# A two-layer relational graph convolution: groups of 512 nodes in a circular buffer of 1536, and steps ordered by tile numbers

## The chip, the cores and the metric

The kernel runs on one core of a Trainium2 chip. The metric is the device time of one execution in microseconds (us). "Before" is the kernel as it stood, "after" is the changed one.

## What is computed

Two layers of a relational graph convolution over N = 50,000 nodes with 128 features, 16 relations and 8 bases, and a layer normalization of the input plus the result. There are 850,000 edges, sorted by destination: 800,000 random ones and a self loop for each node.

```python
def layer(h, src, dst, rel, basis, w_comp, loop_w, bias):
    W = einsum('rb,bio->rio', w_comp, basis)               # 16 matrices of 128x128
    agg = segment_sum(h[src], dst * 16 + rel, 50000 * 16)  # by node and relation
    msg = einsum('nri,rio->no', agg.reshape(50000, 16, 128), W)
    return relu(msg + h @ loop_w + bias)

h = layer(x, src, dst, edge_type_16, basis1, w_comp1, loop_w1, bias1)
h = layer(h, src, dst, edge_type_16, basis2, w_comp2, loop_w2, bias2)
out = layernorm(x + h)
```

The kernel sums by basis rather than by relation: for node n and basis b it needs the sum over n's edges of w_comp[rel, b] * h[src], and multiplies these 8 vectors by the 8 basis matrices.

## The kernel before

**Tiles and chunks.** The edges without the self loops lie in 6250 tiles of P = 128 per layer; K = 10 tiles are a chunk, C = 625 chunks a layer, and a chunk covers about 80 nodes. GpSimd (POOL) fetches the 128 source rows of a tile by an indirect DMA (L231) into `g`. There are GATHERS = 4 buffers of a chunk each. In the round of chunk c the gathers of chunk c + 2 are issued; they go into the buffer that chunk c - 2 had, so they wait for the matmuls that read it.

**Products.** The edges of one tile go to at most WN = 12 neighbouring nodes. For a chunk, VectorE (DVE) makes `own` (L783: does the edge go to node w of the 12, a comparison of `grid` with `key`) and `hot` (L790: `own` times the edge's 8 coefficients `pm`). One matmul per tile (L874) multiplies the 128 gathered rows by the 128 x 96 `hot` and leaves, for 12 nodes and 8 bases, the sums of this tile in `pa`; five tiles (PER) fill a bank of PSUM, and `pa` has three banks. Five tiles later, `add` (L823) has VectorE add the 96 columns to the `ring`, at an offset that it reads from a table into a register. The ring is a circular buffer in SBUF of RING = 1024 nodes with 8 bases each.

**Coefficients.** `weights` makes `pm` for four chunks at a time: a load of the offsets and of the relations by SP's queue, a comparison (L622), and five matmuls (L627) into the PSUM bank `fixed`. This one bank also holds `grid` and, in its last columns, the masks `bit` for the preparation of the edge lists. `hot_of` reads `pm` and `grid` from there.

**Groups.** Nodes are finished in groups of GN = 256 (J = 2), NGR = 196 a layer, of which TURN = 4 fit in the ring. A group goes through two generators:

- `from_itself`, ahead of its first edges, puts the self loops into the ring: loads by SP's queue (L652 for `hT` in layer 2), the comparison `is_lrel` (L655), in layer 1 the transposes of the group's own rows (L661) and a copy by ScalarE (L663), then four pairs of matmuls that repeat the loop's coefficient over the 128 features (L683, into a `po` bank), each followed by a multiplication by `hT` into the ring (L674, VectorE).
- `finish`, when its last chunk is added: in every fourth group the wrap of the ring (L699, L700), the copy of the group's sums by ScalarE into `own` (L705), eight matmuls with the basis matrices into `pn` (L710), one with the loop matrix (L712), the ReLU `oT` by ScalarE (L715), transposes back into `po` (L722), and a copy out by ScalarE (layer 1, L727) or the addition of x and the normalization (layer 2, L730 and `normed`), and the store.

`ps_o` has three `po` banks for both generators, `pn` one bank.

**What sets the order.** On PE, POOL, VectorE and ScalarE the instructions run in the order in which the code issues them (`manual_schedule`). The loop over chunks issues the gathers, then per tile its matmul, the add of the tile five before, and `beside`, which takes one step of the generators at fixed tile numbers of the chunk:

```python
elif t in (0, 5, 7):
    next(owning, None)
if t in (1, 2, 3, 4, 6, 8, 9) and ending:
    if next(ending[0], 0) == 0:
        ending.pop(0)
```

So a step and the one that reads its result mostly stand one to three tiles apart. In layer 1 the loop also takes a step per chunk of `coming`, which prepares later edge lists (`runs`, `loops_of`, `rows_of`) with VectorE, among it predicated copies under the masks `bit` (L311).

Of the kernel before, what the change touches and what calls it, by code (L numbers as in the profile page):

```python
# [30 lines left out]

# [52 lines left out]
def tile_rgcn_resnorm(  # L84
# [23 lines left out]
    TURN = RING // GN  # L108
# [10 lines left out]
    assert D == P and N >= P and edges.shape[0] == 1 and AT * NR == P and PER * NB * WN <= BANK and AT * PER * NB == WEIGHTS and PER == HALF and S <= P and C >= 4 and M > 0 and N % C == 0 and N % J == 0 and 2 * GN == BANK and NB % 2 == 0 and LOOPS <= P and RING % GN == 0 and C % BATCH == 1 and C > 4 * BATCH and RUN - LK // 2 == LIVE and 2 * C <= NG * P and N <= 1 << 16 and E % ROW == 0  # L119
# [16 lines left out]
    ps_c = ctx.enter_context(tc.tile_pool(name="ps_c", bufs=1, space=PSUM))  # L136
# [13 lines left out]
    COMP, BASIS, LOOP, BIAS, EACH, BIAS_OF, SPLIT = [], [], [], [], [], [], []  # L150
# [3 lines left out]
    def weighed():  # L154
# [19 lines left out]
        for n, (basis, w_comp, loop_w, bias) in enumerate(  # L174
            ((basis1, w_comp1, loop_w1, bias1), (basis2, w_comp2, loop_w2, bias2))
        ):
# [3 lines left out]
            wc = consts.tile([P, NR, NB], F32, name=f"comp{n}")  # L180
            nc.scalar.dma_start(
                wc, bass.AP(tensor=w_comp.tensor, offset=w_comp.offset, ap=[[0, P], [NB, NR], [1, NB]])
            )
            COMP.append(wc)
# [3 lines left out]
            b = consts.tile([P, D], F32, name=f"bias{n}")  # L188
            nc.scalar.dma_start(b, bass.AP(tensor=bias.tensor, offset=bias.offset, ap=[[0, P], [1, D]]))
            BIAS.append(b)  # L190
# [64 lines left out]
    first_of = consts.tile([1, C], F32, name="first_of")  # L255
# [189 lines left out]
    def rows_of(j, pool):  # L445
# [83 lines left out]
        yield  # L529

    def count_up(pool):
        last = 5 * NG + len(ROWS)
        off = pool.tile([P, RUN], F32, name="k_f")[0:1, :C]
        even = pool.tile([P, RUN], F32, name="loop_f")[0:1, :C]
        nc.gpsimd.iota(
# [557 lines left out]
```

## Time and profile before

| | before |
|---|---|
| three timed runs | 18257.6, 18254.12, 18248.03 us; median 18254.12 |
| profiled execution | 18432.54 us, its span 18430.7 us |
| granted clock of TensorE | 0.616 |
| TensorE matmuls (PE) busy | 8689.0 us (47%) |
| VectorE (DVE) busy | 7036.3 us (38%) |
| ScalarE (ACT) busy | 1325.2 us (7%) |
| GpSimd (POOL) busy | 11864.9 us (64%) |

How the lines of the profile read: in a group of instructions, "L710 PE MATMUL pn<-own,basis" is line, engine, operation, output and inputs; then the shapes and the count; behind the first bar the busy time and the mean of one in ns; behind the second the idle time of the engine just before these instructions, with what ended most of it. In the answer for one tile, "938/944/1628" are the least, median and longest duration in ns, then the times of the first and last start. A line of the waits has engine, tile and line of the waiting instruction, what it waited for, then the sum in us, the count, and the longest. A line of the timeline has the start in us, the duration, and in square brackets the engine's idle time before it; "remote" is a release that the profile assigns to no instruction of the core, "issue" is time in which the engine waited for nothing that the profile shows.

### The profile page before, as it was taken

Reading aid. Unit: us, or ns where it says so; the run is one execution under the profiler, and the core shown is the slowest. Engines: PE = TensorE matmul, PEld = TensorE weight load, DVE = VectorE, ACT = ScalarE, POOL = GpSimd, SP = SyncE. Lnnn points to the kernel's source line nnn. Section 1 sums busy time; section 2 is a strip of 40 time slices with the busy share of each in tenths; the row PEclk is TensorE's granted clock in tenths of the full one; section 3 lists DMA queues with packets and bytes.
Section 4 is the critical chain, followed back from the end, with each engine's and each line's share of the span. In section 5 each row is a group of like instructions: output and inputs, shape, how many; then the busy total and the mean of one; then the engine's idle time right before and its main releaser. Section 6 shows DMA issues by size and latency. Waiting matters only on the chain.

```text
span 18430.7 us, 149743 instructions
## 1 busy us (share of the span) xinstructions
PE 8689.0 (47%) x39620; PEld 7646.3 (41%) x39620; DVE 7036.3 (38%) x20473; ACT 1325.2 (7%) x1822; POOL 11864.9 (64%) x12531
## 2 busy tenths in 40 slices
PE   3444444444444445444444444444444444444444
PEld 3434344443444444444444444444444444434444
DVE  5444444444333333333333333333333333333333
ACT  0000000000000000000000000000000000000000
POOL 5666666666666666666666666666666666666665
PEclk7666666666666666666656656666565566566666
DMA  2222222222222222222222222222222222222222
GB/s 76 66 66 63 66 67 65 63 66 60 57 58 58 57 58 58 58 58 58 57 54 58 58 58 57 57 58 58 58 57 58 58 58 58 58 57 58 58 58 53
DMA packets 672879, 1096.42 MB, mean 59 GB/s; under 512 B 228802, under 2 KB 460484, under 8 KB 672020
## 3 DMA queue, kind: packets, MB, share of 16 engines
q0 software_dynamic: 403552, 826.82, 18.3%
q1 hardware_dynamic: 264964, 258.48, 4.5%
q8 instruction: 321, 5.26, 0.1%
q14 instruction: 538, 4.41, 0.1%
q10 hardware_dynamic: 3504, 1.45, 0.0%
HBM read 987.91 MB, written 97.93 MB: 59 GB/s over the span
## 4 chain that ended last, share of the span: by engine, by line
another core or an unknown queue 31%; issue 31%; PE 25%; DVE 8%; ACT 3%; DVEq 1%; DMA 1%; POOL 0%; ACTq 0%; SPq 0%; POOLq 0%
PE pa L874 13%; PE pn L710 7%; DVE ring L823 4%; ACT own L705 2%; PE po L683 2%; PE fixed L627 2%; DVE ring L674 1%; PE po L722 1%; PE pn L712 1%; DVEq L817 1%; DVE own L783 0%; POOL g L231 0%; DVE hot L790 0%; ACT oT L715 0%
## 5 line engine op out<-in xcount | busy, mean ns | idle before, releaser
L231 POOL DMA_INDIRECT g<-H,src x6250 | 5906.3, 945 | 3201.9 <-issue 1405.7
L231 POOL DMA_INDIRECT g<-in_x_dram,src x6250 | 5926.1, 948 | 3160.3 <-issue 1390.7
L874 PEld LDWEIGHTS pa<-hot,g 128*128 128x128 f32 x25000 | 5511.7, 286 | 2565.6 <-issue 1651.4
L874 PE MATMUL pa<-hot,g 128*128 128x96 f32 x25000 | 5607.9, 364 | 1941.5 <-issue 1415.6
L823 DVE TENSOR_TENSOR ring<-pa,ring 128x96 f32 x12500 | 3209.7, 257 | 7648.7 <-remote 3719.9
L710 PE MATMUL pn<-own,basis 128*128 128x256 f32 x6208 | 2692.7, 521 | 2918.5 <-issue 1534.5
L710 PEld LDWEIGHTS pn<-own,basis 128*128 128x128 f32 x6208 | 1297.3, 257 | 3040.7 <-issue 1611.0
L683 PE MATMUL po<-is_lrel,split 96*128 96x256 bf16 x3136 | 899.7, 385 | 2937.4 <-issue 1057.7
L683 PEld LDWEIGHTS <-split 96*128 96x128 bf16 x3136 | 444.1, 148 | 3117.8 <-issue 2819.0
L790 DVE TENSOR_TENSOR hot<-fixed,own 128x960 f32<-128x960 f32 x1250 | 1447.1, 1158 | 45.3 <-remote 2.4
L674 DVE TENSOR_TENSOR ring<-po,hT 128x512 f32<-128x512 f32 x1568 | 1081.0, 690 | 625.5 <-remote 190.0
L783 DVE TENSOR_TENSOR own<-fixed,key 128x120 bf16<-128x120 f32 x1250 | 343.6, 275 | 2393.2 <-remote 1125.6
L705 ACT COPY own<-ring 128x2048 f32<-128x2048 f32 x388 | 736.4, 1898 | 5427.0 <-DVE ring L823 4446.7
L722 PE MATMUL po<-ident,oT 128*128 128x128 f32 (+1 forms) x784 | 264.1, 438 | 1562.6 <-issue 792.7
L722 PEld LDWEIGHTS po<-ident,oT 128*128 128x128 f32 (+1 forms) x784 | 129.4, 213 | 1638.8 <-issue 829.9
L627 PE MATMUL fixed<-each,is_rel 128*128 128x64 f32 x3140 | 614.1, 359 | 162.7 <-issue 160.5
L627 PEld LDWEIGHTS fixed<-each,is_rel 128*128 128x128 f32 x3140 | 606.6, 281 | 190.7 <-issue 175.4
L715 ACT ACTIVATE oT<-pn,bias_of 128x256 f32<-128x256 f32 x392 | 185.3, 473 | 6042.7 <-remote 3831.8
L712 PE MATMUL pn<-hT,loop 128*128 128x256 f32 (+1 forms) x784 | 344.2, 520 | 88.7 <-issue 87.9
L663 ACT COPY hT<-po 128x256 f32<-128x256 f32 x196 | 75.7, 386 | 2956.0 <-remote 1772.5
L730 DVE TENSOR_TENSOR t<-po,xw 128x256 f32<-128x256 f32 x196 | 82.5, 421 | 509.9 <-remote 435.3
L712 PEld LDWEIGHTS pn<-hT,loop 128*128 128x128 f32 x784 | 167.1, 257 | 87.8 <-issue 87.4
(126 smaller groups left out, 1804.6 us busy)
## 6 DMA issues: line engine op xcount, KB each, us to landing
g<-in_x_dram,src POOLq DMA_INDIRECT x6250
g<-H,src POOLq DMA_INDIRECT x6250
lrel<-LREL SPq DMA_DIRECT2D x390, 96.0 KB
h_own<-in_x_dram SPq DMA_DIRECT2D x195, 128.0 KB
xw<-in_x_dram SPq DMA_DIRECT2D x195, 128.0 KB
rel<-REL SPq DMA_DIRECT2D x312, 80.0 KB
H1T<-oT SPq DMA_DIRECT2D x195, 128.0 KB
H<-t SPq DMA_DIRECT2D x195, 128.0 KB
```

The costliest lines, as they stand in the source:

```text
L231: return nc.gpsimd.indirect_dma_start(out=to, out_offset=None, in_=of, in_offset=bass.IndirectOffsetOnAxis(ap=idx, axis=0))
L627: nc.tensor.matmul(of[:, :, j * NB : (j + 1) * NB], is_rel[:m, j * P : (j + 1) * P], EACH[n][:m], start=True, stop=True,)
L674: nc.vector.tensor_tensor(ring[:, b - 2 : b, at : at + cnt], pair[:, :, :cnt], hT[:, None, :cnt].to_broadcast([P, 2, cnt]), op=OP.mult,)
L683: nc.tensor.matmul(pair[:, i, :cnt], SPLIT[n][:LOOPS, b + i, :], is_rel[:LOOPS, :cnt], start=True, stop=True,)
L705: nc.scalar.copy(own, ring[:, :, at : at + cnt])
L710: nc.tensor.matmul(pn[:, :cnt], BASIS[n][:, b, :], own[:, b, :], start=b == 0, stop=False)
L712: nc.tensor.matmul(pn[:, :cnt], LOOP[n], hTs.pop(g)[:, :cnt], start=False, stop=True)
L722: nc.tensor.transpose(po[:m, j * D : (j + 1) * D], turned_back[:, j, :], ident)
L783: nc.vector.tensor_tensor(own[:, : ks(c)], grid[:, None, :].to_broadcast([P, ks(c), WN]), key[:, c * K : c * K + ks(c), None].to_broadcast ...
L790: nc.vector.tensor_tensor(hot[:, : ks(c)], pm[:, c % Q * K : c % Q * K + ks(c), :, None].to_broadcast([P, ks(c), NB, WN]), own[:, : ks(c), ...
L823: nc.vector.tensor_tensor(into, pa[:, k % PER * NB * WN : (k % PER + 1) * NB * WN].rearrange("d (b w) -> d b w", w=WN), into, op=OP.add,)
L874: nc.tensor.matmul(pa[:, i * NB * WN : (i + 1) * NB * WN], g[:, k + i, :], hot[:, k + i].rearrange("e b w -> e (b w)"), start=True, stop=True,
```

## The change

- Groups are twice as large, J = 4 and GN = 512, NGR = 98; the ring holds TURN = 3 of them, RING = 1536.
- `fixed` is given up: `grid` is the first 12 columns of a constant in SBUF, `bit` a tile in SBUF, and `pm` is copied by ScalarE from a `po` bank into SBUF (`Weights.kept`). `pa` gets the bank that becomes free, as its fourth.
- The generators are replaced by the classes `Weights` and `Group`, whose steps are methods. Each step is put into a heap under a tile number (`later`), and after each tile's matmul the steps that have come due are issued (`go_on`). `planned` sets the numbers: the multiplication into the ring (`own`) stands BEHIND = 10 tiles behind its matmul (`repeat`), those matmuls APART = 5 tiles apart; the first `base` matmul AFTER = 16 behind the copy of the sums, the next three tiles apart; the ReLU 10 behind `loop`, the transposes (`back`) 16 behind the ReLU, the first step of the store 10 behind those. Loads stand 28 to 44 tiles ahead of their group's or batch's products.
- `add` stands 10 tiles behind its matmul instead of five.
- `Turns.take` hands out `pa` and `po` banks in turn. When all are held, it first issues the reader of the oldest (a `Once`, so it isn't issued again at its own time).
- `hot` has four buffers instead of three, and `hot_of` is issued at a tile number like the other steps. `own` (the sums), `oT`, `xw`, `t`, `h_own`, `lrel` and `is_lrel` have one buffer each.
- Around it: the offset modulo 1536 is worked out with a multiplication and shifts where a mask did for 1024; a check of the chunks' first nodes moves from the end of layer 1 into `rows_of`; constants that only the fallback branch needs are loaded in it (this branch is not taken with these inputs).

The core of the diff:

```diff
-BITS_AT_ONCE = BANK - WEIGHTS - WN
+BITS_AT_ONCE = 224
 GATHERS = 4
-J = 2
+J = 4
 NEAR = 128
 BATCH = 4
-RING = 1024
+TURN = 3
 PARTS = 3
+BEHIND = 10
+AFTER = 16
+APART = 5
...
-    TURN = RING // GN
+    RING = TURN * GN
...
-    fixed = ps_c.tile([P, BANK], F32, name="fixed")
-    grid = fixed[:, WEIGHTS : WEIGHTS + WN]
-    nc.vector.tensor_copy(grid, col[:, :WN])
+    grid = col[:, :WN]
...
-    ps_a = ctx.enter_context(tc.tile_pool(name="ps_a", bufs=3, space=PSUM))
+    ps_a = ctx.enter_context(tc.tile_pool(name="ps_a", bufs=4, space=PSUM))
...
+    class Turns:
+        def __init__(self, pool, name, count):
+            self.pool, self.name, self.count, self.held = pool, name, count, []
+        def take(self, read=None):
+            if len(self.held) == self.count:
+                first = self.held.pop(0)
+                if first is not None:
+                    first()
+            self.held.append(read)
+            return self.pool.tile([P, BANK], F32, name=self.name)
+    class Once:
+        def __init__(self, what, *args):
+            self.what, self.args = what, args
+        def __call__(self):
+            what, self.what = self.what, None
+            if what is not None:
+                what(*self.args)
+    sums_a, sums_o = Turns(ps_a, "pa", 4), Turns(ps_o, "po", 3)
...
-    bit = fixed[:, WEIGHTS + WN :].bitcast(I32)
+    bit = consts.tile([P, BITS_AT_ONCE], I32, name="bit")
...
+            class Weights:
+                def __init__(self, c, n):
+                    self.c, self.n = c, n
+                    self.m = min(AT, 2 * (C - c)) * NR
+                    self.keep = Once(self.kept)
...
+                def multiply(self):
+                    m = self.m
+                    self.po = sums_o.take(self.keep)
+                    of = self.po[:, :WEIGHTS].rearrange("e (t j) -> e t j", t=AT)
+                    for j in range(PER):
+                        nc.tensor.matmul(
+                            of[:, :, j * NB : (j + 1) * NB],
+                            self.is_rel[:m, j * P : (j + 1) * P],
+                            EACH[self.n][:m],
+                            start=True,
+                            stop=True,
+                        )
+                def kept(self):
+                    pm = hp.tile([P, WEIGHTS], F32, name="pm", bufs=1)
+                    nc.scalar.copy(pm, self.po[:, :WEIGHTS])
+                    self.pm = pm.rearrange("e (t b) -> e t b", b=NB)
...
+            class Group:
+                def __init__(self, g, of, n, copied):
+                    self.g, self.of, self.n, self.copied = g, of, n, copied
+                    self.m, self.cnt = nodes(g), nodes(g) * J
+                    self.at = g % TURN * GN
+                    self.each, self.made = {}, False
+                    self.keep, self.kept = Once(self.turned), Once(self.store, 0)
+                    self.owns = [Once(self.own, b) for b in range(NB)]
...
+                def repeat(self, b):
+                    cnt = self.cnt
+                    self.each[b] = sums_o.take(self.owns[b])
                     nc.tensor.matmul(
+                        self.each[b][:, :cnt],
+                        SPLIT[self.n][:LOOPS, b, :],
+                        self.is_rel[:LOOPS, :cnt],
                         start=True,
                         stop=True,
                     )
+                def own(self, b):
+                    cnt = self.cnt
+                    assert self.g < TURN or self.copied[0] > self.g - TURN
+                    nc.vector.tensor_tensor(
+                        ring[:, b, self.at : self.at + cnt],
+                        self.each.pop(b)[:, :cnt],
+                        self.hT[:, :cnt],
+                        op=OP.mult,
+                    )
+                    self.made = b == NB - 1
...
+                def planned(self, later, free):
+                    from_chunk = -(-(self.g * GN - NEAR) // (N // C)) - 1
+                    start = K * from_chunk - 4
+                    end = max(K * final(self.g) + K - 1 + BEHIND, free - AFTER + 1)
+                    went = start - APART * NB - BEHIND
+                    later(went - 28, self.load)
+                    if self.n == 0:
+                        later(went - 18, self.turn)
+                        later(went - 10, self.keep)
+                    later(went - 10, self.compare)
+                    for b in range(NB):
+                        later(went + APART * b, self.repeat, b)
+                        later(went + APART * b + BEHIND, self.owns[b])
+                    later(end, self.copy)
+                    for b in range(NB):
+                        later(end + AFTER + 3 * b, self.base, b)
+                    end += AFTER + 3 * NB
+                    later(end, self.loop)
+                    later(end + BEHIND, self.relu)
+                    later(end + BEHIND + AFTER, self.back)
+                    later(end + 2 * BEHIND + AFTER, self.kept)
+                    for step in range(1, 3 if self.n else 1):
+                        later(end + 2 * BEHIND + AFTER + 3 * step, self.store, step)
+                    return end + BEHIND
...
-                def hot_of(c, pm):
+                def hot_of(c):
+                    pm = batches[c // BATCH].pm
...
-                    hot = hp.tile([P, K, NB, WN], F32, name="hot", bufs=3)
+                    hot = hp.tile([P, K, NB, WN], F32, name="hot", bufs=4)
...
+                hots, behind, copied, events = {}, [], [0], []
+                def added_up_to(i):
+                    while behind and behind[0][0] <= i + BEHIND:
+                        add(*behind.pop(0)[1])
+                def later(time, what, *args):
+                    heapq.heappush(events, (time, len(order), what, args))
+                    order.append(None)
+                order = []
+                def go_on(now):
+                    while events and events[0][0] <= now:
+                        _, _, what, args = heapq.heappop(events)
+                        what(*args)
+                batches = [Weights(c, n) for c in range(0, C, BATCH)]
+                batches[0].load()
+                batches[0].compare()
+                batches[0].multiply()
+                batches[0].keep()
                 for c in range(C):
+                    if c >= 2:
+                        later(K * (c - 2) + PER, hot_of, c)
+                for batch in batches[1:]:
+                    when = K * (batch.c - 3) + PER + 3
+                    later(when - 44, batch.load)
+                    later(when - 28, batch.compare)
+                    later(when - AFTER, batch.multiply)
+                    later(when, batch.keep)
+                groups = [Group(g, of, n, copied) for g in range(NGR)]
+                free = 0
+                for one in groups:
+                    free = one.planned(later, free)
...
+                    for k in range(K):
+                        if k % PER == 0:
+                            pa = sums_a.take(Once(added_up_to, c * K + k + PER - 1))
+                        if k < ks(c):
+                            nc.tensor.matmul(
+                                pa[:, k % PER * NB * WN : (k % PER + 1) * NB * WN],
+                                g[:, k, :],
+                                hot[:, k].rearrange("e b w -> e (b w)"),
+                                start=True,
+                                stop=True,
+                            )
+                            behind.append((c * K + k + BEHIND, (c, k, pa)))
+                        added_up_to(c * K + k - BEHIND)
+                        if c or k >= BEHIND - 2:
+                            go_on(c * K + k)
...
+                now = C * K
+                while events or behind:
+                    added_up_to(now - BEHIND)
+                    go_on(now)
+                    now += 1
```

More of the change, by code (lines that the diff above doesn't have):

```diff
@@ new lines, in base, with loop @@
+                def base(self, b):
+                    if b == 0:
+                        self.pn = ps_n.tile([P, BANK], F32, name="pn")
+                    nc.tensor.matmul(
+                        self.pn[:, : self.cnt], BASIS[self.n][:, b, :], self.sums[:, b, :], start=b == 0, stop=False
+                    )
+                def loop(self):
+                    nc.tensor.matmul(
+                        self.pn[:, : self.cnt], LOOP[self.n], self.hT[:, : self.cnt], start=False, stop=True
+                    )
@@ new lines, in chunked @@
+                for batch in batches[1:]:
[6 more added lines that the diff above has]
+                free = 0
+                for one in groups:
+                    free = one.planned(later, free)
+                for c in range(C):
```

399 lines of the change are left out of this document (160 added, 239 removed).

## The prediction

> **What bounds the kernel now.** I read the page first, for what each engine has to do.
>
> ```profile
> span 18430.7 us, 149743 instructions
> ...
> PE 8689.0 (47%) x39620; PEld 7646.3 (41%) x39620; DVE 7036.3 (38%) x20473; ACT 1325.2 (7%) x1822; POOL 11864.9 (64%) x12531
> ...
> L231 POOL DMA_INDIRECT g<-H,src x6250 | 5906.3, 945 | 3201.9 <-issue 1405.7
> L231 POOL DMA_INDIRECT g<-in_x_dram,src x6250 | 5926.1, 948 | 3160.3 <-issue 1390.7
> ...
> L874 PE MATMUL pa<-hot,g 128*128 128x96 f32 x25000 | 5607.9, 364 | 1941.5 <-issue 1415.6
> ...
> L710 PE MATMUL pn<-own,basis 128*128 128x256 f32 x6208 | 2692.7, 521 | 2918.5 <-issue 1534.5
> ...
> L683 PE MATMUL po<-is_lrel,split 96*128 96x256 bf16 x3136 | 899.7, 385 | 2937.4 <-issue 1057.7
> ...
> L790 DVE TENSOR_TENSOR hot<-fixed,own 128x960 f32<-128x960 f32 x1250 | 1447.1, 1158 | 45.3 <-remote 2.4
> ...
> L783 DVE TENSOR_TENSOR own<-fixed,key 128x120 bf16<-128x120 f32 x1250 | 343.6, 275 | 2393.2 <-remote 1125.6
> L705 ACT COPY own<-ring 128x2048 f32<-128x2048 f32 x388 | 736.4, 1898 | 5427.0 <-DVE ring L823 4446.7
> L722 PE MATMUL po<-ident,oT 128*128 128x128 f32 (+1 forms) x784 | 264.1, 438 | 1562.6 <-issue 792.7
> ```
>
> GpSimd (POOL) has the most work: 12,500 gathers of one 128-edge tile each, 5906.3 + 5926.1 = 11832.4 us, but it is busy for 64% only. TensorE (PE) is busy for 47%, 8689.0 / 12,500 = 0.695 us per tile. Nothing is full, so something waits. The answer for the tile `g` tells where the gathers begin and end, and the list of waits who waits.
>
> ```profile
> L231 POOL DMA_INDIRECT g<-in_x_dram,src x6250: 938/944/1628, 49.2 to 9279.9; - x196
> L231 POOL DMA_INDIRECT g<-H,src x6250: 938/944/1257, 9319.5 to 18388.7; - x196
> ```
>
> ```profile
> ACT oT L715 <- remote: 3831.8, 161, 40.9
> DVE ring L823 <- remote: 3719.9, 583, 33.3
> ...
> POOL g L231 <- remote: 1886.2, 1437, 5.8
> ...
> POOL g L231 <- PE pa L874: 1217.7, 1452, 6.4
> ```
>
> The timeline of some 15 us in layer 2 shows both a running GpSimd and a pause of it.
>
> ```profile
> 12011.92 0.62 PE L712 MATMUL pn<-hT,loop 128*128 128x256 f32 x2
> ...
> 12014.33 0.94 POOL L231 DMA_INDIRECT g<-H,src  x1 [0.30 <-issue]
> ...
> 12015.58 0.94 POOL L231 DMA_INDIRECT g<-H,src  x1 [0.30 <-issue]
> ...
> 12016.71 0.24 PE L874 MATMUL pa<-hot,g 128*128 128x96 f32 x1 [0.49 <-issue]
> 12016.83 0.94 POOL L231 DMA_INDIRECT g<-H,src  x1 [0.30 <-issue]
> ...
> 12018.08 0.94 POOL L231 DMA_INDIRECT g<-H,src  x1 [0.30 <-issue]
> ...
> 12019.32 0.94 POOL L231 DMA_INDIRECT g<-H,src  x1 [0.30 <-issue]
> ...
> 12020.57 0.94 POOL L231 DMA_INDIRECT g<-H,src  x1 [0.30 <-PE pa L874]
> 12024.76 0.32 SPq L652 DMA_DIRECT2D hT<-H1T  x1
> 12024.77 0.47 ACT L715 ACTIVATE oT<-pn,bias_of 128x256 f32<-128x256 f32 x1 [20.61 <-remote]
> 12024.79 0.94 POOL L231 DMA_INDIRECT g<-H,src  x1 [3.28 <-remote]
> ...
> 12025.30 0.70 PE L722 MATMUL po<-ident,oT 128*128 128x128 f32 x2 [5.43 <-ACT oT L715]
> ```
>
> From 12014.33 to 12019.32 there are four steps of 1.248 us: that is GpSimd's own pace. 12,500 x 1.248 = 15,600 us. Before the first gather lie 49.2 us, between the layers 9319.5 - 9279.9 - 1.2 = 38.4, after the last 18430.7 - 18388.7 - 1.2 = 40.8, together 128 us. The rest, 18430.7 - 15,600 - 128 = **2702 us, is pauses of GpSimd**, 0.216 us per gather. The list gives them to TensorE (1217.7) and to "remote" (1886.2, the 0.30 us that every gather has included): a gather overwrites the buffer of the chunk four before, so it waits until TensorE is done with that. TensorE, some 40 tiles behind, is late.
>
> Why is it late with work for 47%? The same rows show it. The last matmul of `pn` (L712) is done at 12012.54 by its row; its reader, the ReLU at L715, starts at 12024.77, 12.2 us later, within 0.03 us of a DMA queue and a gather that also waited for TensorE. TensorE's completions came late and together, at the end of a pause of GpSimd, and meanwhile its own matmuls crawled (half a microsecond of "issue" before the one at 12016.71). Then it stood 5.43 us for that ReLU, before the transposes at L722. The next rows show the same with another reader.
>
> ```profile
> 12035.10 0.36 PE L874 MATMUL pa<-hot,g 128*128 128x96 f32 x2
> ...
> 12043.47 0.26 DVE L823 TENSOR_TENSOR ring<-pa,ring 128x96 f32 x1 [10.12 <-remote]
> ...
> 12046.00 1.90 ACT L705 COPY own<-ring 128x2048 f32<-128x2048 f32 x1 [14.66 <-DVE ring L823]
> ...
> 12047.95 1.22 PE L710 MATMUL pn<-own,basis 128*128 128x256 f32 x2 [12.49 <-issue]
> ```
>
> TensorE falls silent at 12035.46; VectorE gets the product 8 us later (10.12 us of "remote"), finishes the group's last adds, ScalarE copies the group's sums (`own`, 1.90 us) until 12047.90, and only then do the `pn` matmuls start: 12.49 us without a matmul. Where no gather runs the lag is gone:
>
> ```profile
> 18388.73 0.94 POOL L231 DMA_INDIRECT g<-H,src  x1 [0.30 <-issue]
> ...
> 18410.82 0.62 PE L712 MATMUL pn<-hT,loop 128*128 128x256 f32 x2
> ...
> 18411.48 0.47 ACT L715 ACTIVATE oT<-pn,bias_of 128x256 f32<-128x256 f32 x1 [9.47 <-PE pn L712]
> ```
>
> Here L715 follows L712's end (18411.44) by 0.04 us. So the bound is a loop of TensorE, its readers and TensorE again, with up to 12 us from a result to its reader, and GpSimd pays for it. TensorE's idle time, 18430.7 - 8689.0 = 9742 us, by the last column of its rows: before L683 2937, before L710 2919, before L722 1563, together 7419 or 76%; before the products themselves (L874) 1942, 20%.
>
> **The change, part by part.**
>
> *Ten or more tiles between a result and its reader.* All that the 76% wait for moves away: the multiplication of the ring by VectorE stands 10 tiles behind its matmul (`repeat`, `own`), the copy of the sums 16 tiles ahead of `base`, the ReLU 10 behind `loop`, the transposes 16 behind that, the adds 10 behind the products (5 before), with a fourth bank for those. At GpSimd's pace 10 tiles are 12.5 us and 16 are 20.0, against a lag of 12.2 and a copy of 2 x 1.898 = 3.8 us. What is queued behind a late reader is then not TensorE. TensorE needs 0.695 us per tile of the 1.248 that GpSimd takes, so it can catch up, and the 40 tiles of lead hide single delays. If pauses go as TensorE's idle time does, 76% go, those before its small rows with them, and the 20% before L874 stay: 2702 x 0.20 = 540 us. That is the forecast's largest unknown. Its bounds are 0 (all hidden) and 2702 (completions stay late because gathers run); I take 540, since the row it comes from is the only idle time whose cause the change doesn't move.
>
> *Groups of 512 in a ring of 1536.* Half as many copies, comparisons, ReLUs and SP transfers of twice the length, the same columns through TensorE with half the weight loads. All lie beside the gathers, under TensorE's 0.55 us of slack per tile; 0 us as long as GpSimd is the bound. If it is not, TensorE's work is no larger than now. SP's queue gets fewer loads, issued 28 to 44 tiles ahead. At the end of each layer the last groups' copy and `base` steps are twice as long with nothing to hide them: between 0 and the whole present tail of 40.8 us for each layer, 40 us taken for both.
>
> *Weights, grid and bit masks from PSUM to SBUF.* The copy of the weights (`kept`) goes to ScalarE, which works 7% of the time. But `hot` (L790) and `own` (L783) now read both inputs from SBUF. Of today's rows the preparation in layer 1 does that, and there the gathers are longer (longest 1628 ns, median 944). The first and last of its 14 costly groups, of 112 us together in the first 5000 us, and the two costliest of the predicated copies that get a second SBUF input (their first is a mask in `fixed`):
>
> ```profile
> L311 DVE COPY_PREDICATED l_word<-fixed,l_word 128x180 int32<-128x180 int32 x260 | 93.4, 359 | 14.9 <-DVE fixed L308 2.8 <-remote 1.9 <-issue 1.5
> ...
> L311 DVE COPY_PREDICATED word<-fixed,word 128x180 int32<-128x180 int32 x180 | 64.7, 359 | 6.1
> ...
> L344 DVE SCALAR_TENSOR_TENSOR word<-loop_f,k_f 128x672 uint8<-128x672 f32 x10 | 9.1, 908 | 0.3
> ...
> L490 DVE TENSOR_TENSOR l_word<-word,begin 128x640 f32<-128x640 uint16 x8 | 6.5, 817 | 0.0
> ```
>
> Layer 1's gathers took 5926.1 - 5906.3 = 19.8 us more than layer 2's, 0.18 us for each us of such work. `hot` and `own` are 1447.1 + 343.6 = 1790.7 us: 0.18 x 1790.7 = 320 us on GpSimd's path; the masks 0.18 x (93.4 + 64.7) = 28, call it 30. The ends are 0 and 1790.7; the 0.18 is the nearest row, of the same form of instruction beside the same gathers. Below 0 is excluded: a gather doesn't get shorter than its 944 ns. The Trainium skill ("SBUF — State Buffer", section "Who interferes with whom") speaks against this part: a VectorE instruction with two SBUF inputs takes the interface that it shares with GpSimd, exclusively for its whole length, and the other engine blocks. By that the 112 us should have cost up to 112; the trace shows 19.8, a sixth. What it would make of the sum is rival B.
>
> *The sum*: 15,600 + 128 + 40 + 320 + 30 + 540 = 16,658 us of span, and 1.8 around it (18432.5 against 18430.7): 16,660. The median of the runs stands at 18254.12 / 18432.54 = 0.9903 of the profiled one; so **16,500 us**. Between no pauses left (16,120, so 15,960) and pauses of 1040 us (17,160, so 17,000) I call it the forecast's own range: 15,950 to 17,000.
>
> **Rivals.**
>
> A. *Completions stay late.* The lag ends when GpSimd pauses (12024.76 to 12024.79), and is missing without gathers (18411.48). If TensorE can't retire its results while gathers run, distance helps only until its own queue is full; and the distance is in tiles: when TensorE catches up at 0.695 us per tile, ten tiles are 7 us, less than 12.2. For it: the crawling matmuls. Against: the four gathers from 12014.33 on each needed a result of TensorE and got it in time, so completions do come through, only late. Half of the pauses, 1350 us: 16,658 + 810 = 17,470, so 17,300 us. Chance 0.20, for 17,000 to 17,900.
>
> B. *The shared interface.* Each `hot` and `own` stops the gathers for its length whenever one runs, 11832 / 15,600 = 76% of the time: 1790.7 x 0.76 = 1361 instead of 320, so 17,700 and 17,530 us. The mechanism is the one that the page of the Trainium skill cited above states. Against it: the 19.8 us. Chance 0.08.
>
> C. *The bank of the other steps (slower).* The three `po` banks are now taken in turn by weights, ring and transposes. A product of the weights holds its bank for 16 tiles, but takes come every 5 tiles while a group is repeated, so the third take comes round after 15: `take` then calls the reader early, and the matmul behind it, with all products in TensorE's queue, stands until ScalarE has read. That is 10 to 15 tiles after the product, 12.5 us or more, just above the lag; with a TensorE that catches up it is below. If each of the 196 groups exposes one lag of 12.2 us, 2391 us come on top: 19,050, so 18,870 us. It decides from some 148 exposures (1805 us) on. Chance of slower by this: 0.16.
>
> D. *It doesn't do what it says*: the pauses change their releaser and not their sum, 18,220 to 18,290 us. The steps do stand apart in the program, so 0.04.
>
> **How the numbers follow.** Forecast 0.46, still faster (no pauses and no cost of the interface) 0.04, A 0.20, B 0.08: faster 0.78; D 0.04 as the same, C 0.16, and 0.02 for the upper end of A at no gain, which makes the same 0.06. About 0.2%, 36 us, is what the measurement can tell from no change. The range reaches from 15,950 over A and B to 18,290, the edge of "slower", and leaves out 0.04 below and 0.16 above.
>
> **What would show it.** Right: GpSimd's share rises from 64% to 72% or more, and the rows of ring, `base` and transposes lose most of the 7419 us before them while L874 keeps or gains; the waits of ScalarE and VectorE for "remote" may stay as long, since nothing waits behind them. The port: mean `g` of both layers at 0.97 us rather than 0.945. A: GpSimd still under 70%, its pauses with TensorE as releaser, matmuls of L874 with "issue" before them. B: `g` near 1.05 us. C: idle time of TensorE before products ended by ScalarE's copy of the weights. The forecast is wrong if pauses stay above 1040 us, or if gathers take over 0.99 us.

## The result and the profile after

The changed kernel takes 18,090.45 us in the median against 18,251.07 us: ratio 0.9912, 95% interval 0.9895 to 0.9929. It is faster by 161 us, where 1,754 us were forecast. The profiled execution of after took 18,092.07 us, its span is 18,090.2.

The kernel before was measured again with every experiment, on eight chips, and took 15,786 to 15,820 us there; so each time below stands beside that of the kernel before on the same chip.

First the page of after: busy times, then groups (busy, mean ns, idle time before them and what ended most of it).

```profile
span 18090.2 us, 137615 instructions
...
PE 8815.7 (49%) x34524; PEld 6699.9 (37%) x34524; DVE 6821.1 (38%) x19683; ACT 1346.6 (7%) x1452; POOL 12297.6 (68%) x12540
...
L247 POOL DMA_INDIRECT g<-in_x_dram,src x6250 | 6140.9, 983 | 2844.0 <-issue 1397.4
L247 POOL DMA_INDIRECT g<-H,src x6250 | 6120.1, 979 | 2864.0 <-issue 1410.5
L961 PE MATMUL pa<-hot,g 128*128 128x96 f32 x25000 | 5476.4, 355 | 4369.5 <-issue 3768.7
...
L754 PE MATMUL pn<-own,basis 128*128 128x512 f32 x3104 | 2296.2, 818 | 529.6 <-issue 515.5
L720 PE MATMUL po<-is_lrel,split 96*128 96x512 bf16 x1568 | 797.8, 510 | 2312.8 <-issue 903.2
...
L655 PE MATMUL po<-each,is_rel 128*128 128x64 f32 x3140 | 671.9, 375 | 1159.1 <-issue 727.1
...
L778 PE MATMUL po<-ident,oT 128*128 128x128 f32 (+1 forms) x784 | 205.6, 397 | 650.2 <-DVE ring L731 388.9
```

The answer for the tile `g` of after (least, median and longest ns, first and last start):

```profile
L247 POOL DMA_INDIRECT g<-in_x_dram,src x6250: 938/945/1929, 45.8 to 9064.3; - x196
L247 POOL DMA_INDIRECT g<-H,src x6250: 938/945/1932, 9099.2 to 18049.3; - x196
```

Two things moved. The gathers got longer: 6140.9 + 6120.1 = 12,261.0 us against 12,500 x 0.944 = 11,800, so 461 us where before had 32; the median is the same, the longest is 1.93 us. And GpSimd's pauses shrank. The same sum splits every span: 12,499 steps of 1.248 us = 15,599; what the gathers are longer; what lies before the first and after the last start; and the rest, pauses, with the stop between the layers among them. Before: 15,599 + 32 + 91 + **2,708**; after: 15,599 + 461 + 87 + **1,944**. So the pauses gave 764 us and the longer gathers took 429 back. Of the 340 us between the two spans the timed runs show 161, because the profiled execution of before lay 181 us above its median.

TensorE's idle time went where the prediction's steps pointed, and came back elsewhere. Before the repeats, `base` and the transposes it fell from 2,937 + 2,919 + 1,563 = 7,419 us to 2,313 + 530 + 650 = 3,493. Before the products it rose from 1,942 to 4,370, before the weights' products from 163 to 1,159. In all 18,090.2 - 8,815.7 = 9,274 us are left of 9,742. The new idle time is "issue": TensorE waits for nothing that the profile names. The timeline of PE in after shows what it looks like:

```profile
7198.48 0.37 PE L961 MATMUL pa<-hot,g 128*128 128x96 f32 x1
7200.29 0.32 PE L961 MATMUL pa<-hot,g 128*128 128x96 f32 x1 [1.45 <-issue]
7201.69 0.59 PE L720 MATMUL po<-is_lrel,split 96*128 96x512 bf16 x1 [1.08 <-issue]
7204.49 0.32 PE L961 MATMUL pa<-hot,g 128*128 128x96 f32 x1 [2.21 <-issue]
7205.89 0.32 PE L961 MATMUL pa<-hot,g 128*128 128x96 f32 x1 [1.08 <-issue]
```

From the second on, the starts are 1.40, 2.80 and 1.40 us apart, multiples of 0.70. It is so in the whole trace: of the 3,958 steps of 1 to 6 us from one start of TensorE to the next, 60% lie within 0.03 us of a multiple of 0.70. The profile names no reader in front of these matmuls, and no cause.

### The profile page after: what moved, and what is told of

The parts are those of the page before. It is cut to its first block, busy times and chain, and to the rows that moved or that the text cites. A ratio compares the mean times of both kernels' runs of the same rounds, so it can differ in the third digit from the quotient of the medians.

```text
span 18090.2 us, 137615 instructions
## 1 busy us (share of the span) xinstructions
PE 8815.7 (49%) x34524; PEld 6699.9 (37%) x34524; DVE 6821.1 (38%) x19683; ACT 1346.6 (7%) x1452; POOL 12297.6 (68%) x12540
## 4 chain that ended last, share of the span: by engine, by line
issue 39%; PE 28%; another core or an unknown queue 15%; DVE 8%; POOL 6%; DMA 2%; ACT 1%; DVEq 1%; POOLq 0%; ACTq 0%; SPq 0%
PE pa L961 16%; PE pn L754 7%; POOL g L247 6%; DVE ring L897 4%; PE po L655 2%; DVE ring L731 2%; PE po L720 1%; DMA g<-in_x_dram,src 1%; DVEq L891 1%; DMA g<-H,src 1%; ACT own L748 1%; PE po L778 1%; PE pn L759 1%; DVE own L870 0%
## 5 line engine op out<-in xcount | busy, mean ns | idle before, releaser
L961 PEld LDWEIGHTS pa<-hot,g 128*128 128x128 f32 x25000 | 5222.6, 274 | 8042.2 <-issue 7000.4
L247 POOL DMA_INDIRECT g<-in_x_dram,src x6250 | 6140.9, 983 | 2844.0 <-issue 1397.4
L247 POOL DMA_INDIRECT g<-H,src x6250 | 6120.1, 979 | 2864.0 <-issue 1410.5
L754 PE MATMUL pn<-own,basis 128*128 128x512 f32 x3104 | 2296.2, 818 | 529.6 <-issue 515.5
L720 PE MATMUL po<-is_lrel,split 96*128 96x512 bf16 x1568 | 797.8, 510 | 2312.8 <-issue 903.2
L877 DVE TENSOR_TENSOR hot<-pm,own 128x960 f32<-128x960 f32 x1250 | 1451.4, 1161 | 81.1 <-ACT pm L665 13.8
L655 PE MATMUL po<-each,is_rel 128*128 128x64 f32 x3140 | 671.9, 375 | 1159.1 <-issue 727.1
L655 PEld LDWEIGHTS po<-each,is_rel 128*128 128x128 f32 x3140 | 625.5, 289 | 1209.5 <-issue 747.3
L748 ACT COPY own<-ring 128x4096 f32<-128x4096 f32 x194 | 699.5, 3606 | 3877.3 <-DVE ring L897 2158.7
L754 PEld LDWEIGHTS pn<-own,basis 128*128 128x128 f32 x3104 | 668.4, 253 | 768.6 <-issue 766.5
L870 DVE TENSOR_TENSOR own<-col,key 128x120 bf16<-128x120 f32 x1250 | 346.4, 277 | 0.5
L759 PE MATMUL pn<-hT,loop 128*128 128x512 f32 x392 | 265.6, 759 | 32.5 <-issue 32.2
```

What stands on the lines that cost most here:

```text
L247: return nc.gpsimd.indirect_dma_start(out=to, out_offset=None, in_=of, in_offset=bass.IndirectOffsetOnAxis(ap=idx, axis=0))
L655: nc.tensor.matmul(of[:, :, j * NB : (j + 1) * NB], self.is_rel[:m, j * P : (j + 1) * P], EACH[self.n][:m], start=True, stop=True,)
L720: nc.tensor.matmul(self.each[b][:, :cnt], SPLIT[self.n][:LOOPS, b, :], self.is_rel[:LOOPS, :cnt], start=True, stop=True,)
L748: nc.scalar.copy(self.sums, ring[:, :, at : at + cnt])
L754: nc.tensor.matmul(self.pn[:, : self.cnt], BASIS[self.n][:, b, :], self.sums[:, b, :], start=b == 0, stop=False)
L759: nc.tensor.matmul(self.pn[:, : self.cnt], LOOP[self.n], self.hT[:, : self.cnt], start=False, stop=True)
```

## The experiments

Theory 1: while gathers run, TensorE's semaphore increments are delivered late and slowly, and fewer of them mean fewer pauses. Theory 2: TensorE is slow for another reason, and the late increments are only its sign.

**few2 and few: fewer increments.** Products in reverse order, adds by banks, in few2 with one tiny matmul per chunk that waits for all ten gathers.

```diff
+    if k == 0:                                       # few2 alone
+        nc.tensor.matmul(pa[:1, 480 : 480 + K], ones[:, 0:1], g[:, :, 0], start=True, stop=True)
-    nc.tensor.matmul(pa[...], g[:, k, :], hot[:, k]...)
+    nc.tensor.matmul(pa[...], g[:, K - 1 - k, :], hot[:, K - 1 - k]...)
...
-    add(*behind.pop(0)[1])
+    for one in reversed(bank):
+        add(*one[1])
```

> The changed kernel with fewer semaphore increments of TensorE, 6,473 in the program instead of 16,703: the ten products of a chunk run in reverse order behind one tiny matmul that waits for all ten gathers, and the five adds of a bank start with the one whose product came last, so that nobody waits for a single product any more. Nothing of the work is left out. Theory 1 (while gathers run, TensorE's increments are delivered late and at a limited rate, and everything queues behind them): pauses of GpSimd fall from some 1,900 to under 700 us, 16,500 to 16,900 us. Theory 2 (TensorE itself is slow, by its half clock or by its waits for the gathers, and the increments are only a sign of it): 17,900 to 18,200 us.

> As few2 without the tiny matmul: the products of a chunk in reverse order, adds by banks, 10,452 increments of TensorE in the program, since the matmuls that wait for a gather of their own keep theirs. Theory 1: between the changed kernel and few2, about 17,200 us. Theory 2: as the changed kernel, 17,900 to 18,200 us.

Measured: few2 16,419 us and few 16,332 us, beside a kernel before of 15,813 (few2: ratio 1.0382, 1.0365 to 1.0400). few2 lies a little under theory 1's range and few 868 us under its 17,200, but neither says anything for it: the kernel before didn't have the pauses here.

**nogather and decoupled.**

```diff
-    for k in range(ks(to)):                                       # nogather
+    for k in range(ks(to) if n == 0 and to < GATHERS else 0):
...
-    g[:, k, :],                                                   # decoupled
+    ident,
```

> The changed kernel without its gathers but for the first 40 tiles; all products are made of those rows again and again. The program has 3,605 increments of TensorE. Theory 1 (gathers are what delays TensorE): TensorE's 8,800 us of work with little idle time, 9,500 to 12,000 us, no matmuls 0.7 us apart. Theory 2 in the form that TensorE crawls by itself: over 15,000 us.

> The changed kernel with all gathers, but the products read a constant tile in place of the gathered rows, so neither engine waits for the other (3,581 increments of TensorE). Theory 1: GpSimd runs at its own pace, 15,600 us and the dearer gathers, and TensorE, with few increments, keeps up: 16,000 to 16,500 us. Theory 2 in the form that a running GpSimd slows TensorE's instructions whatever they signal: TensorE ends well behind the gathers, over 17,500 us.

Measured: 8,851 us and 16,450 us. Without gathers everything else needs 8,851 us (at a granted clock of 0.782, where after has 0.609), less than expected: GpSimd's 15,599 us give the other engines nearly 1.8 times what they need. In decoupled, TensorE's busy tenths in 40 slices of the span show that it is done after 26 of them:

```profile
PE   4454343443888887777777777400000000000000
```

The gathers alone set 16,450 us. No gather waits for a matmul there, and of the 850 us of the span over 15,599, their own length is 742.

**after2 and before2: the two kernels once more.** No edit.

> The changed kernel once more, beside the runs of few2, in which the kernel before took 15,813 us and not 18,251. Theory 3 (the gathers' own length: VectorE's hot and own with both inputs in SBUF lengthen the gathers beside them, by some 430 to 560 us, and pauses of GpSimd are what else differs): where the kernel before takes 15,813 us, few pauses are left to take away, and the changed kernel is slower, 16,300 to 16,450 us; where before takes 18,250 us, 18,090 us again. Theory 1 (spaced steps are a gain by themselves): at or below the kernel before in both cases.

> The kernel before with a profile. Theory 3: gathers of 945 ns with next to none longer; if it takes 15,813 us, TensorE's results reach their readers without the 12 us lag and GpSimd's pauses are under 150 us; if 18,250 us, pauses of 2,700 us as in the first profile.

Measured: 16,198 us against 15,820, ratio 1.0236 (1.0219 to 1.0253): on this chip the change makes the kernel slower, though 102 us under theory 3's lower end, 16,300. before2 was profiled at 15,786 us. Its page, and its timeline at one `pn` group:

```profile
span 15784.1 us, 149743 instructions
...
L231 POOL DMA_INDIRECT g<-in_x_dram,src x6250 | 5924.4, 948 | 1935.8 <-issue 869.2
L231 POOL DMA_INDIRECT g<-H,src x6250 | 5912.1, 946 | 1923.3 <-issue 888.0
...
L710 PE MATMUL pn<-own,basis 128*128 128x256 f32 x6208 | 2868.3, 557 | 48.8 <-ACT own L705 48.8
...
L722 PE MATMUL po<-ident,oT 128*128 128x128 f32 (+1 forms) x784 | 239.2, 406 | 3.3 <-ACT oT L715 3.3
```

```profile
10032.72 0.62 PE L712 MATMUL pn<-hT,loop 128*128 128x256 f32 x2
10033.38 0.47 ACT L715 ACTIVATE oT<-pn,bias_of 128x256 f32<-128x256 f32 x1 [20.04 <-PE pn L712]
10033.59 0.95 POOL L231 DMA_INDIRECT g<-H,src  x1 [0.30 <-PE pn L712]
```

The same instructions in the same order, with gathers running: the ReLU starts 0.04 us after the last `pn` matmul where the prediction's rows had 12.2. TensorE stands 49 us for the sums and 3 us for the ReLU in the whole run, where it stood 2,919 and 1,563. The pauses are 75 us. TensorE's increments can be matched with their matmuls in the stretches between two idle times of 2 us or more in which the records have as many of the one as of the other. In before2 that is so for 10,578, and they come 0.013 to 0.016 us after the end of the matmul. In before it is so for only 404, with a median of 5.0 us, and one in ten over 12.5 us. The granted clock isn't what differs: 0.616 in before, 0.594 in before2. And the matmuls' starts lose their grid: in after2, 3% of 3,053 steps lie within 0.03 us of a multiple of 0.70. So the lag that the whole forecast rests on belongs to the recorded measurement, not to the kernel's order.

What is left is theory 3, the price of the SBUF inputs. The two `g` rows of after2:

```profile
L247 POOL DMA_INDIRECT g<-in_x_dram,src x6250 | 6137.9, 982 | 1934.8 <-issue 1011.5
L247 POOL DMA_INDIRECT g<-H,src x6250 | 6112.3, 978 | 1929.7 <-issue 1045.9
```

6137.9 + 6112.3 - 11,800 = 450 us longer (before2: 37), with 80 us of pauses (before2: 75): the loss is the gathers' length, to within 15 us.

**sbuf_only: that part alone, in the kernel before.** The masks stay in PSUM.

```diff
-    grid = fixed[:, WEIGHTS : WEIGHTS + WN]
+    grid = col[:, :WN]
...
-    yield pm.rearrange("e (t b) -> e t b", b=NB)
+    kept = hp.tile([P, WEIGHTS], F32, name="pm", bufs=1)
+    nc.scalar.copy(kept, pm)
+    yield kept.rearrange("e (t b) -> e t b", b=NB)
```

> The kernel before with one part of the change: the weights are copied by ScalarE from their PSUM bank into SBUF and the grid is read from SBUF, so that hot and own have both inputs in SBUF; masks, groups, ring, distances and banks as before. Theory 3: the gathers grow by some 350 to 450 us in all, nearly all of it beside hot. Where the kernel before takes 15,820 us: 16,170 to 16,270 us, the whole loss of the changed kernel. Where it takes 18,250 us: 18,550 to 18,700 us if the longer gathers come on top, 18,200 to 18,400 if the pauses shrink by as much. Rival (the loss is from another part): 15,820 and 18,250.

Measured: 16,251 us against 15,789, ratio 1.0295 (1.0278 to 1.0312); gathers 502 us longer, pauses 76. This one part alone costs 462 us, where the whole change cost 378 in after2.

**psum, hot_psum: that part undone, and hot's half of it.**

```diff
-    pm = hp.tile([P, WEIGHTS], F32, name="pm", bufs=1)
+    pm = fixed[:, :WEIGHTS]
-    sums_a = Turns(ps_a, "pa", 4)
+    sums_a = Turns(ps_a, "pa", 3)
...
-    grid = col[:, :WN]                                  # psum alone, and bit likewise
+    grid = fixed[:, WEIGHTS : WEIGHTS + WN]
```

> The changed kernel with weights, grid and masks back in one PSUM bank (ScalarE copies the weights from their po bank into it), and so three product banks instead of four; groups, ring and the order of the steps as changed. Theory 3: gathers at 945 ns again, 430 to 560 us less than the changed kernel on the same chip: 15,780 to 15,850 us where before takes 15,813, and 17,600 to 17,800 where it takes 18,250. Rival (the long gathers come from the doubled groups or the ring, not from the SBUF inputs): no change against the changed kernel.

> The changed kernel with the weights alone in a PSUM bank (and so three product banks, the preparation's transposes in the po banks, a chunk's hot made before the next weights are kept); grid and masks stay in SBUF, so that own still has both inputs in SBUF and hot has not. Theory 3, by instruction: the 332 to 335 us beside hot go, and some 50 to 120 us of excess stay: 15,830 to 15,920 us where before takes 15,800; some 17,700 us where it takes 18,250, or 18,000 if the pauses grow by it. Rival (own and the masks matter as much as hot): above 16,000 us.

Measured: psum 15,847 us against 15,820, ratio 1.0017 (1.0008 to 1.0027), gathers 82 us longer. In psum two chunks of layer 1 read weights that the next batch had replaced already; instructions and sizes are the same, and hot_psum makes these chunks' `hot` first. hot_psum, with the preparation's transposes in `po` banks as well: 15,824 us against 15,788, 6 us under the range expected, gathers 65 us longer though `own` and the masks stay in SBUF. So it is `hot`.

**near: short distances.**

```diff
-BEHIND = 10
-AFTER = 16
+BEHIND = 3
+AFTER = 4
```

> The changed kernel with short distances: readers 3 tiles behind their results instead of 10, and 4 where it has 16; groups, ring, SBUF inputs and four product banks as changed. Where the kernel before takes 15,820 us, TensorE's results reach their readers within 0.02 us and the distances are worth nothing: 16,150 to 16,300 us. Where it takes 18,250 us, theory 1 (distances hide part of the late results): 18,500 to 19,200 us, against 18,090 for the changed kernel; the rival (the 765 us less of pauses come from fewer increments and larger groups): 18,000 to 18,200 us.

Measured: 16,265 us (before 15,789), with 80 us of pauses as in after2 and gathers 513 us longer. Where results arrive at once the distances are worth nothing as waits. On another chip (near_b) 16,274 us, beside 15,809:

> near once more, on another chip, for the case of late completions: 18,500 to 19,200 us if the distances are what saved 765 us of pauses, 18,000 to 18,200 if they are not; 16,150 to 16,300 us where before takes 15,790.

**before_few and best_ok: fewer increments, without the price of the SBUF inputs.** before_few is the edit of few2 in the kernel before; best_ok is few2 with psum's bank, the preparation's transposes in `po` banks, and `hot` of a chunk made before the weights that replace its own.

> The kernel before with the products of a chunk in reverse order behind one tiny matmul, and adds by banks of five: 5,712 increments of TensorE in the program instead of 18,683; groups, ring, generators and PSUM as before. Where the kernel before takes 15,800 us: the same within 50 us, since GpSimd's own pace is all. Where it takes 18,250 us and TensorE's results come late: theory 1 (the number of results that somebody waits for sets how much) 16,000 to 17,000 us; theory 2, 17,900 to 18,400 us.

> The changed kernel with weights, grid and masks in one PSUM bank, products in reverse order, adds by banks, 5,900 increments of TensorE; a chunk's hot is made before the next weights are kept. Where before takes 15,800 us: 15,780 to 15,860 us. Where it takes 18,250 us: theory 1 15,900 to 16,800, theory 2 17,500 to 17,800 us.

Measured: 15,796 and 15,819 us, beside 15,789; before_few on another chip (before_few_b) 15,791 beside 15,790:

> before_few once more, on another chip, for the case of late completions: 16,000 to 17,000 us if the number of increments that somebody waits for sets how late they come, 17,900 to 18,400 if not; 15,800 us where before takes 15,790.

few_psum and best, psum with the fewer increments of few and few2, have psum's fault in two and five chunks; they took 15,847 us beside 15,820 and 15,822 beside 15,789, as expected for results that come at once. Prompt everywhere, so theories 1 and 2 stay untested. No version beats the kernel before here: best_ok's 15,817 us of span are 15,599 of pace, 41 of longer gathers, 87 outside and 90 of pauses.

**hot_twice: the suspected cost doubled.**

```diff
+    for _ in range(2):
         nc.vector.tensor_tensor(hot[...], pm[...], own[...], op=OP.mult)
```

> The changed kernel with each hot written twice in a row by the same VectorE instruction, both inputs in SBUF: the suspected cost doubled, the output the same. In the changed kernel gathers of over 1 us beside hot carry 332 to 335 us of excess. Theory 3: some 330 us more, 16,450 to 16,650 us where before takes 15,800 us, with gathers of up to 3.1 us; where it takes 18,250 us, 18,300 to 18,500 us if the excess comes on top and 18,090 to 18,200 if the pauses of GpSimd shrink by it. Rival (VectorE's load, not its inputs): the same rise without longer single gathers.

Measured: 16,165 us against 15,787: no rise over after2, gathers 406 us longer, though VectorE works 2,912.5 us on `hot` instead of 1,451.4. A miss, and the most useful one. The timeline of after2 at one `hot`, then of hot_twice:

```profile
9768.51 1.16 DVE L877 TENSOR_TENSOR hot<-pm,own 128x960 f32<-128x960 f32 x1
9768.56 1.93 POOL L247 DMA_INDIRECT g<-H,src  x1 [0.30 <-issue]
```

```profile
9171.95 0.94 POOL L247 DMA_INDIRECT g<-H,src  x1 [0.30 <-DMA g<-H,src]
9173.11 2.35 DVE L878 TENSOR_TENSOR hot<-pm,own 128x960 f32<-128x960 f32 x2
9173.20 1.88 POOL L247 DMA_INDIRECT g<-H,src  x1 [0.30 <-PE pa L962]
9175.39 0.94 POOL L247 DMA_INDIRECT g<-H,src  x1 [0.30 <-PE pa L962]
```

In after2 `hot` ends at 9769.67 and the gather that started inside it at 9770.49, 0.82 us later: it stood at its beginning, for the first 0.12 of its 0.94 us, until `hot` was over. Over all 1,250 `hot` of after2, each of the 485 gathers that start 0.1 to 1.0 us after the start of `hot` takes over 1 us and ends 0.81 to 0.85 us after it, and none of the 622 that start up to 0.2 us before it takes over 1 us. In hot_twice the gather gets in between the two instructions (the first ends at about 9174.27, the gather at 9175.08), and the next starts when the second is as good as over. Hence theory 4: a gather caught at its start waits for the instruction that runs, and no more. How many are caught depends on where the gathers happen to fall: beside `hot`, 541 take over 1 us in after2, 557 in hot_twice, but 923 in after, 948 in sbuf_only and 1,027 in few2, whose gathers are 644 us longer in all.

**hot_split: the same work in five pieces.**

```diff
-    nc.vector.tensor_tensor(hot[:, : ks(c)], pm[...], own[...], op=OP.mult)
+    for k in range(0, ks(c), 2):
+        nc.vector.tensor_tensor(hot[:, k : k + 2], pm[...], own[...], op=OP.mult)
```

> The changed kernel with hot made in five pieces of two tiles each instead of one instruction of ten; all else as changed, both inputs still in SBUF. Theory 4 (a gather that starts while hot runs stands at its beginning until that instruction has ended, and one that has started isn't touched; so the price is one remaining instruction length for each gather caught, not a share of VectorE's time): a piece takes some 0.25 us, a gather is held 0.1 us on average, and the 335 us beside hot become 60 to 110: gathers up to 1.3 us, 15,870 to 15,970 us where before takes 15,790. Theory 3 as the prediction had it (0.18 us per us of such work): no change, 16,150 to 16,300 us. Where before takes 18,250 us: 17,750 to 17,900 if the price is on top of the pauses, 18,000 to 18,150 if the pauses take it up.

Measured: 15,939 us against 15,790, ratio 1.0094 (1.0077 to 1.0111). Its rows:

```profile
L247 POOL DMA_INDIRECT g<-in_x_dram,src x6250 | 6008.9, 961 | 1933.5 <-issue 1020.0
L247 POOL DMA_INDIRECT g<-H,src x6250 | 5973.3, 956 | 1927.9 <-issue 1048.1
...
L879 DVE TENSOR_TENSOR hot<-pm,own 128x192 f32<-128x192 f32 x6250 | 1799.9, 352 | 78.9 <-ACT pm L665 16.0
```

Both inputs are still in SBUF and VectorE works 348 us more on `hot`, yet the gathers are 6008.9 + 5973.3 - 11,800 = 182 us longer instead of 450. The time is in theory 4's range; less the 65 us that hot_psum keeps, 117 us lie beside `hot`, a little over the 60 to 110 expected. A share of VectorE's time is excluded.

## Why the prediction was wrong, step by step

**The bound.** The lines were read rightly and taken for the wrong thing. "Completions came late and together" was true of that trace, and no part of the profile said why. Nor is its "remote" a cause: the trace has 16,041 of the 18,412 increments of TensorE's matmuls and 8,827 of VectorE's 19,756 (before2: 18,398 and 19,746), so a wait can be "remote" because the increment that ended it isn't on record. The prediction made it a loop of TensorE and its readers, which the order of steps could open. The same program with its completions on time needs 15,784 us: the 2,708 us of pauses were hardly the order's doing.

**The step that failed** is "if pauses go as TensorE's idle time does, 76% go": 540 us of pauses were to be left, 1,944 are (some 1,910 without the stop between the layers, which the prediction has among its 128). The rows lost a little over half of their idle time (7,419 to 3,493 us); but most of that went to the products and the weights' products instead of leaving, 1,942 to 4,370 and 163 to 1,159. So these two traces read as if a wait taken off an engine whose own results are late finds the next place to stand. This is what rival A forecast, with its signs (GpSimd at 68%, under 70; "issue" before the products, 1,416 to 3,769 us). Its price was too small: half of the pauses were to stay, 72% did. Its reason, that results are late because gathers run, isn't borne out: in before2 the gathers run and the results are prompt. What the 764 us less came from, the distances or the 2,009 fewer increments (16,403 for 18,412) or the larger groups, isn't shown.

**The SBUF inputs** were put at 320 + 30 = 350 us and measured 429 in the recorded pair, 413 in after2 and 466 in sbuf_only. The size was near by luck, the working wrong: 0.18 us for each us of such work would have made hot_twice some 260 us dearer. The Trainium skill ("SBUF — State Buffer", section "Who interferes with whom"), which the prediction set aside at a sixth of its price, was right for the single instruction: the other engine is shut out until it ends. The trace agrees for a gather caught at its start, which ends some 0.82 us after `hot`. What makes the sum small is that only the start of a gather is hit; rival B's 1,361 us counted every overlap.

**The ends** were to cost 40 us and cost none: outside the gathers 91 us became 87, between the layers 39.6 became 34.9.

**The scale.** 0.9903 between the median and the profiled execution was carried over to after, whose profiled execution lies at its median (18,092 and 18,090): 160 us too few.

**Rivals C and D** didn't happen. The wait that C needs, TensorE before a matmul into `po` for ScalarE's copy of the weights, is there in the list of waits of after, 410 us in these two lines, far from the 1,805 us from which C decides:

```profile
PE po L720 <- ACT pm L665: 276.3, 77, 13.1
...
PE po L778 <- ACT pm L665: 133.6, 31, 12.7
```

Had the completions been prompt, the steps for the rest hold: no pauses to win, 413 us of longer gathers, slower by 2.4%.

**Open.** Why TensorE's completions were late in the recorded measurement; none of the eight chips of the experiments did it, and which chip the recorded pair ran on isn't on record. near_b and before_few_b were run for that and met prompt completions. So what the distances are worth where results come late is untested.

## What to carry to other kernels

A wait whose cause the profile doesn't name ("remote", "issue", a result that lies for microseconds) is no term to be planned away: first see it in a second measurement of the same program, on another chip. When an engine has a pace of its own (here 12,500 x 1.248 us), split the span into pace, longer steps and pauses before pricing a change; what lengthens a step of the pace counts in full, and pauses may not be there tomorrow. Keep one input of a long VectorE instruction out of SBUF beside a running GpSimd, or cut it in pieces.

## What was not expected of the hardware

- TensorE's increments come 0.012 to 0.017 us after the matmul in the traces of all eight chips, where they can be matched, and 5.0 us after it in the median of the first trace; in after's, many matmuls start 1.40 or 2.80 us apart. The same program took 18,251 us and 15,790 us.
- A gather is held in its first 0.12 us or so while VectorE runs an instruction with two SBUF inputs, and takes 0.82 us more once that has ended; the longest took 1.93 us, beside a `hot` of 1.16. The short `own` (0.27 us), which runs just before `hot`, does the same: of 93 gathers in after2 that start 0.2 to 0.4 us before `hot`, 21 take over 1 us, by about 0.09 us too long, and those that start 0.05 to 0.1 us into `own` end 0.81 to 0.82 us after it. With `grid` in PSUM, in psum, none of the 88 such gathers takes over 1 us.
- Twice the work in two instructions holds no more gathers than once: 406 us against 450.
